# A third layer issued in program order on four engines, with the ends of its passes spread over the steps that follow

## Chip, core and metric

One Trainium2 chip, one core. The metric is the device time of one execution in microseconds (us). Before any experiment the kernel before took 2380.44 us (median of 3 runs, 2375.94 to 2380.57). Stage lengths come from the profiled execution of each kernel, times and ratios from all of its runs.

## The reference, cut to what matters

Four layers work on 4096 nodes of 128 features with a full 4096 x 4096 matrix `adj`; each adds to x and normalises it. The change concerns the third layer, an attention with four heads, and the product with `adj` that starts the fourth.

```python
def _L2_gnn_ref(x, adj_matrix, weight, att_src, att_dst, bias):      # third layer
    ...
    C = alpha_src[None, :, :] + alpha_dst[:, None, :]
    adj_t = adj_matrix.T[..., None]
    tau = adj_t * jnp.exp(jnp.maximum(0.2 * C, C))
    tau_sum = jnp.sum(tau, axis=1, keepdims=True)
    att_weights = tau / tau_sum
    z = jnp.einsum('mnh,nhf->mhf', adj_t * att_weights, h_prime)
    return z.reshape(n, heads * f_out) + bias

def _L3_gnn_ref(h, adj, W_self, W_neigh):                            # fourth layer
    deg = jnp.clip(jnp.sum(adj, axis=1, keepdims=True), 1.0)
    h_neigh = adj @ h / deg
    return h @ W_self + h_neigh @ W_neigh
...
    x = _layernorm(x + _L2_gnn_ref(...), axis=-1)
    x = _layernorm(x + _L3_gnn_ref(...), axis=-1)
```

The denominators are sums of tau; the numerators need adj * tau, that is, a second factor of `adj`. Both are products on TensorE.

## The kernel before

The third layer takes the targets in four strips of 1024 (`WB`) and the heads in two pairs: eight passes of 32 steps (`NT`), 128 source nodes a step. (PSUM, below, is the memory in which the results of matmuls stand; the other tiles lie in SBUF.) One step, and the end of a pass:

```python
def attention(l2w, bufs, mp, hp):
    D = []                                            # targets: TensorE spreads them into PSUM
    ...
    for nt in range(NT):
        ...                                           # every second step loads a chunk of adj
        nc.scalar.activation(sq, a[:, 0:OWN], AF.Square)
        for h in range(2):
            nc.vector.scalar_tensor_tensor(tau[:, h, :], D[h], E(h), a, op0=ALU.max, op1=ALU.mult)
        nc.vector.scalar_tensor_tensor(tau2[:, 0, 0:OWN], D[0][:, 0:OWN], E(0), sq,
                                       op0=ALU.max, op1=ALU.mult)                # the 704-wide one
        nc.gpsimd.tensor_tensor(tau2[:, 0, OWN:WB], tau[:, 0, OWN:WB], a[:, OWN:WB], ALU.mult)
        nc.gpsimd.tensor_tensor(tau2[:, 1, :], tau[:, 1, :], a, ALU.mult)
        product(den, nt, tau, True)                   # four matmuls, each on 32 columns
        late.append((nt, tau2))
        if len(late) > 1:
            product(num, *late.pop(0), False)         # numerators one step behind
        yield
    ...                                               # end of the pass: copy, transpose, divide, add to x
```

One matmul of the fourth layer's product (a "piece") is put into each step, and whatever a strip needs at its end is written down in one lump:

```python
for mp in range(NW):
    for hp in range(H // 2):
        if (mp, hp) != (0, 0):                        # pass 0 runs inside the second layer
            for _ in attention(l2w, 3, mp, hp):
                next(pieces, None)
    for _ in pieces:
        pass
    for j in (2 * mp, 2 * mp + 1):
        layer3_block(j)                               # layer norm of the strip, blocks for the product
    pieces = layer3_product(mp)
for _ in pieces:
    pass
```

A scheduler then decides in which order each engine takes its instructions.

## Time and profile before

I cut every profile at the same events: the start of VectorE's 704-wide instruction, which stands once in every step. "Pass 0 ends" is the start of the last one of pass 0; the "edge" runs from there to the first one of pass 1; the "passes" from there to the last one of pass 7; the "tail" from there to the end of the span.

| kernel before | us |
|---|---|
| pass 0 ends | 1482.8 |
| edge from pass 0 to pass 1 | 8.1 |
| passes 1 to 7 (224 steps) | 796.8 |
| tail | 88.6 |
| profiled span | 2376.4 |

### The profile page before, as it was taken

What the parts mean: (1) busy time and instruction counts of PE and PEld (TensorE: products, weight loads), DVE (VectorE), ACT (ScalarE), POOL (GpSimd) and SP (SyncE); (2) the same over time, 40 slices, a digit from 0 to 9 for tenths busy, and PEclk for the clock granted to TensorE, in tenths of its full rate; (3) what the DMA queues carried; (4) which work ended last, traced back from release to release, by engine and by line L of the source; (5) the groups of instructions that cost most, each with busy time, mean ns of one, the idle gap of its engine ahead of it and who ended that gap; (6) DMA issues with size and microseconds to landing.
All of it is one profiled execution on the core that took longest, in us unless ns stands there. A gap on an engine that the chain in (4) does not pass through costs nothing.

```text
span 2376.4 us, 23290 instructions
## 1 busy us (share of the span) xinstructions
PE 2247.5 (95%) x8798; PEld 860.8 (36%) x8798; DVE 1371.0 (58%) x1981; ACT 484.2 (20%) x716; POOL 847.5 (36%) x541
## 2 busy tenths in 40 slices
PE   5899999999999999999999998879998999999988
PEld 3334444444444444444433332112222222222233
DVE  4443458777110110000156656999799999999965
ACT  5665000000000000000122121223222222322220
POOL 0000000000000000000043424999698899889950
PEclk8899999999999999999999998999999999999999
DMA  9988888999878778888877774446665666666655
GB/s 363 347 274 263 246 246 263 290 294 291 263 243 264 233 233 261 280 263 258 262 256 235 266 265 160 146 156 229 213 213 195 209 216 231 212 217 229 220 193 188
DMA packets 261802, 575.39 MB, mean 242 GB/s; under 512 B 9776, under 2 KB 15920, under 8 KB 261680
## 3 DMA queue, kind: packets, MB, share of 16 engines
q1 hardware_dynamic: 252352, 566.27, 73.3%
q10 hardware_dynamic: 9328, 7.54, 1.0%
q8 instruction: 71, 1.16, 0.2%
q14 instruction: 51, 0.42, 0.1%
HBM read 571.67 MB, written 2.10 MB: 241 GB/s over the span
## 4 chain that ended last, share of the span: by engine, by line
PE 83%; DVE 9%; DMA 4%; issue 2%; ACT 1%; POOL 1%; DVEq 0%; ACTq 0%; POOLq 0%
PE pacc L455 27%; PE pacc L319 10%; PE den L607 10%; PE pp L677 10%; PE pp L712 10%; PE num L607 7%; DVE tau L623 5%; DMA chunk<-in_adjT 3%; PE pmm L496 2%; PE num L677 1%; PE px L103 1%; PE pden L305 1%; DVE tau L624 1%; PE ptr L314 1%; PE px L663 1%
## 5 line engine op out<-in xcount | busy, mean ns | idle before, releaser
L623 DVE SCALAR_TENSOR_TENSOR tau<-d,es,chunk 128x1024 f32<-128x1024 f32 x512 | 634.9, 1277 | 25.1 <-issue 16.2
L627 POOL TENSOR_TENSOR tau<-tau,chunk 128x1024 f32<-128x1024 f32 x256 | 611.4, 2388 | 54.8 <-DVE tau L623 47.1
L607 PE MATMUL den<-tau,cs 128*32 128x512 f32 x2048 | 457.5, 605 | 8.6 <-DVE tau L623 8.1
L585 POOL TENSOR_TENSOR x<-x,B2R 128x512 f32<-128x512 f32 x8 | 10.1, 1268 | 1245.1 <-PE px L103 1245.1
L607 PE MATMUL num<-tau,hc 128*32 128x512 f32 x2048 | 413.8, 601 | 32.1 <-POOL tau L627 27.6
L618 ACT ACTIVATE sq<-chunk 128x704 f32<-128x704 f32 x256 | 201.5, 791 | 605.6 <-DVE tau L624 528.9
L626 POOL TENSOR_TENSOR tau<-tau,chunk 128x320 f32<-128x320 f32 x256 | 226.0, 883 | 115.7 <-PE num L607 46.9
L319 PE MATMUL pacc<-chunk,hw 128*128 128x512 f32 x512 | 254.8, 635 | 3.0 <-DVE hw L352 3.0
L677 PE MATMUL pp<-chunk,xT 128*128 128x512 f32 x448 | 243.5, 637 | 11.8 <-DMA chunk<-in_adjT 11.4
L624 DVE SCALAR_TENSOR_TENSOR tau<-d,es,sq 128x704 f32<-128x704 f32 x256 | 241.8, 944 | 18.9 <-PE num L607 14.1
L712 PE MATMUL pp<-chunk,w 128*128 128x512 f32 x512 | 235.6, 602 | 1.2 <-DVE t2T L718 1.2
L455 PE MATMUL pacc<-chunk,x 128*128 128x512 f32 x512 | 223.6, 594 | 0.0
L455 PE MATMUL pacc<-chunk,t 128*128 128x512 f32 x512 | 223.6, 592 | 0.0
L455 PE MATMUL pacc<-chunk,v 128*128 128x512 f32 x512 | 221.4, 592 | 0.0
L607 PEld LDWEIGHTS num<-tau,hc 128*32 128x32 f32 x2048 | 82.2, 109 | 248.2 <-POOL tau L627 83.5
L607 PEld LDWEIGHTS den<-tau,cs 128*32 128x32 f32 x2048 | 86.0, 108 | 222.3 <-issue 106.0
L299 DVE TENSOR_SCALAR pos<-chunk 128x2048 bf16<-128x2048 f32 x92 | 110.8, 1222 | 75.4 <-DMA chunk<-in_adjT 69.6
L517 DVE COPY w<-ptr 128x512 f32<-128x512 f32 x8 | 5.5, 692 | 246.1 <-PE ptr L515 246.1
L455 PEld LDWEIGHTS pacc<-chunk,v 128*128 128x128 f32 x512 | 97.1, 190 | 121.5 <-issue 121.5
L455 PEld LDWEIGHTS pacc<-chunk,t 128*128 128x128 f32 x512 | 96.1, 190 | 114.8 <-issue 114.8
L712 PEld LDWEIGHTS pp<-chunk,w 128*128 128x128 f32 x512 | 92.2, 190 | 124.6 <-issue 117.7
L455 PEld LDWEIGHTS pacc<-chunk,x 128*128 128x128 f32 x512 | 95.8, 190 | 113.4 <-issue 113.4
(171 smaller groups left out, 1461.1 us busy)
## 6 DMA issues: line engine op xcount, KB each, us to landing
chunk<-in_adjT SPq DMA_DIRECT2D x412, 1024.0 KB, 5.5
chunk<-in_adj SPq DMA_DIRECT2D x128, 1024.0 KB, 5.3
xT<-in_xT ACTq DMA_DIRECT2D x8, 256.0 KB, 6.6
out<-o ACTq DMA_DIRECT2D x8, 256.0 KB, 3.6
W1A<-in_w1a ACTq DMA_DIRECT2D x1, 384.0 KB, 3.5
W1B<-in_w1b ACTq DMA_DIRECT2D x1, 384.0 KB, 4.4
W0T<-in_w0gT ACTq DMA_DIRECT2D x1, 64.0 KB, 4.0
W<-in_w0g ACTq DMA_DIRECT2D x1, 64.0 KB, 6.5
```

The costliest lines, as they stand in the source:

```text
L299: nc.vector.tensor_scalar(pos, a, 0.0, None, op0=ALU.is_gt)
L319: nc.tensor.matmul(p, hw[:, j * TB + k, :], a[:, k, :], start=first and k == 0, stop=last and k == TB - 1)
L455: nc.tensor.matmul(p, stationary(c * TB + k), a[:, k, :], start=n == 0 and k == 0, stop=n == NB - 1 and k == TB - 1)
L496: nc.tensor.matmul(ph, W1A[:, k, hh * P:(hh + 1) * P], r, start=k == 0, stop=k == 2)
L607: nc.tensor.matmul(acc[q:q + 32, :], weights(nt, 2 * hp + h, is_den), r[:, h, mb * IB:(mb + 1) * IB], start=nt == 0, stop=nt == NT - 1)
L618: nc.scalar.activation(sq, a[:, 0:OWN], AF.Square)
L623: nc.vector.scalar_tensor_tensor(tau[:, h, :], D[h], E(h), a, op0=ALU.max, op1=ALU.mult)
L624: nc.vector.scalar_tensor_tensor(tau2[:, 0, 0:OWN], D[0][:, 0:OWN], E(0), sq, op0=ALU.max, op1=ALU.mult)
L626: nc.gpsimd.tensor_tensor(tau2[:, 0, OWN:WB], tau[:, 0, OWN:WB], a[:, OWN:WB], ALU.mult)
L627: nc.gpsimd.tensor_tensor(tau2[:, 1, :], tau[:, 1, :], a, ALU.mult)
L677: nc.tensor.matmul(p, y[:, (2 * mp + c) * TB + k, :], a[:, k, :], start=c == 0 and k == 0, stop=c == 1 and k == TB - 1)
L712: nc.tensor.matmul(p, w[:, c * TB + k, :], a[:, k, :], start=c == 0 and k == 0, stop=c == NB - 1 and k == TB - 1)
```

## The change

Its intent: VectorE is to work without a hole through the seven passes. Four engines take their instructions in program order; denominators are multiplied one step behind, numerators two; the stages that end a pass become generators, of which one stage is issued per step of the next pass; the matmuls of the product are dealt out by a credit. The core of the diff, cut:

```diff
+            with tc.manual_schedule(engines={PE, DVE, Activation, Pool}):       # names shortened
+                chains = deque([heads.finish()])
+                pieces = deque()
+                credit = rate = 0.0
...
+                for s, (mp, hp, nt) in enumerate(steps):
+                    if nt == 0:
+                        heads.targets()
+                    a, sq = ahead
+                    tau, tau2 = heads.step(nt, l2w, (3, 4), a, sq)
+                    if s + 1 < len(steps):
+                        ahead = passes[steps[s + 1][:2]].squares(steps[s + 1][2], l2w, 3)
+                    behind.append((heads, nt, tau, tau2))
+                    if len(behind) > 1:
+                        before = behind[-2]
+                        before[0].product(True, before[1], before[2])
+                    if len(behind) > 2:
+                        before = behind.popleft()
+                        before[0].product(False, before[1], before[3])
+                        if before[1] == NT - 1:
+                            ...                # queue the pass end, the strip's layer norm, its product
+                    credit = min(credit + rate, 2.0)
+                    while credit >= 1.0:
+                        credit -= 1.0
+                        if one(pieces):
+                            credit = 0.0
+                    one(chains)
...
-                            if k < TB - 1:
-                                yield
-                        if c == 0:
-                            yield
+                            yield c == 1 and k == TB - 1
...
-                    yield
+                    yield True
...
+                nc.vector.scalar_tensor_tensor(tau[:, 0, :], D[0], E(nt, 0), a, op0=ALU.max, op1=ALU.mult)
+                nc.gpsimd.tensor_tensor(tau2[:, 0, OWN:WB], tau[:, 0, OWN:WB], a[:, OWN:WB], ALU.mult)
+                nc.vector.scalar_tensor_tensor(tau2[:, 0, 0:OWN], D[0][:, 0:OWN], E(nt, 0), sq,
+                                               op0=ALU.max, op1=ALU.mult)
+                nc.vector.scalar_tensor_tensor(tau[:, 1, :], D[1], E(nt, 1), a, op0=ALU.max, op1=ALU.mult)
+                nc.gpsimd.tensor_tensor(tau2[:, 1, :], tau[:, 1, :], a, ALU.mult)
```

The layer norm now takes a strip of eight 128-node tiles at once (`layer3_blocks`):

```python
nc.vector.tensor_scalar_add(s, mv[:, tb, 1], LN_EPS)
nc.scalar.activation(s, s, AF.Sqrt)
yield
nc.vector.reciprocal(s, s)
nc.vector.scalar_tensor_tensor(m, mv[:, tb, 0], -1.0, s, op0=ALU.mult, op1=ALU.mult)
```

## The prediction

> **What bounds the kernel now.** I read the page for the engines' shares, then the table by stretches cut at the edges of the attention passes, then the timeline inside one pass, at one edge between passes and after the last pass. The page names TensorE, but its busy time alone does not settle who sets the pace.
>
> ```profile
> PE 2247.5 (95%) x8798; PEld 860.8 (36%) x8798; DVE 1371.0 (58%) x1981; ACT 484.2 (20%) x716; POOL 847.5 (36%) x541
> L627 POOL TENSOR_TENSOR tau<-tau,chunk 128x1024 f32<-128x1024 f32 x256 | 611.4, 2388 | 54.8 <-DVE tau L623 47.1
> ```
>
> The third layer has eight passes (four target strips, two head pairs) of 32 steps. A step is three VectorE instructions (two tau of 128x1024, one squared part of 128x704), two GpSimd products, four denominator and four numerator matmuls. Pass 0 runs inside the second layer; passes 1 to 7 are the stretches from 1491 to 2288; the last product follows.
>
> ```profile
> core 0: us, PE busy (x) PEld busy (x) DVE busy (x) ACT busy (x) POOL busy (x), PEclk, DMA share, GB/s
> 1137.00:1454.00 317.00, 313.77 (x1087) 121.16 (x1091) 169.38 (x286) 64.36 (x110) 104.30 (x63) 0.99 0.77 254
> 1491.00:1592.00 101.00, 84.21 (x498) 16.03 (x500) 101.00 (x94) 24.51 (x31) 99.78 (x63) 1.00 0.49 156
> 1592.00:1714.00 122.00, 113.82 (x600) 29.89 (x596) 108.28 (x121) 36.20 (x59) 102.25 (x66) 0.99 0.61 209
> 1714.00:1829.00 115.00, 103.13 (x602) 26.96 (x604) 105.78 (x99) 28.22 (x38) 104.21 (x68) 1.00 0.65 217
> 1829.00:1949.00 120.00, 115.43 (x618) 31.29 (x614) 110.88 (x124) 33.25 (x54) 104.04 (x67) 0.99 0.60 204
> 1949.00:2059.00 110.00, 107.52 (x591) 26.89 (x584) 107.15 (x103) 26.40 (x34) 103.85 (x66) 1.00 0.66 229
> 2059.00:2178.00 119.00, 114.44 (x618) 31.37 (x616) 112.25 (x126) 33.36 (x54) 104.65 (x68) 1.00 0.64 214
> 2178.00:2288.00 110.00, 107.54 (x590) 27.02 (x588) 107.17 (x103) 25.62 (x33) 103.86 (x67) 1.00 0.66 227
> 2288.00:2376.00 88.00, 71.82 (x208) 32.81 (x202) 41.12 (x180) 10.07 (x30) 2.26 (x1) 0.92 0.53 170
> ```
>
> To see: pass 1, without pieces of the last product, has VectorE busy all of its 101 us. The other six take 110 to 122 us for about the same VectorE work. VectorE sums to 752.5 of 797 us over the seven, so **44.5 us of idle VectorE** is what reordering can win there. Before 1454 TensorE is full (313.8 of 317); after 2288 it idles 16 of 88 us.
>
> ```profile
> 1533.04 0.95 DVE L624 SCALAR_TENSOR_TENSOR tau<-d,es,sq 128x704 f32<-128x704 f32 x1
> 1533.20 2.37 POOL L627 TENSOR_TENSOR tau<-tau,chunk 128x1024 f32<-128x1024 f32 x1
> ...
> 1536.28 0.95 DVE L624 SCALAR_TENSOR_TENSOR tau<-d,es,sq 128x704 f32<-128x704 f32 x1
> ```
>
> A step is 3.24 us: 1.19 + 1.19 + 0.86 from start to start (the printed 1277 and 944 ns contain an end that overlaps the next). GpSimd needs 2.33 + 0.82 = 3.15 us, nearly the same.
>
> ```profile
> 1713.87 0.95 DVE L624 SCALAR_TENSOR_TENSOR tau<-d,es,sq 128x704 f32<-128x704 f32 x1
> 1722.37 1.28 DVE L623 SCALAR_TENSOR_TENSOR tau<-d,es,chunk 128x1024 f32<-128x1024 f32 x1 [7.56 <-issue]
> ```
>
> An edge between passes: VectorE stands 7.6 us. From the last 704-wide instruction of a pass to the first of the next it is 8.1, 6.3, 12.3, 6.5, 6.4, 6.3 and 6.4 us, where 3.24 would be one step. Inside passes 2, 4 and 6 there are more holes, early, where the layer norm and the blocks for the product are made.
>
> ```profile
> 2287.74 0.94 DVE L624 SCALAR_TENSOR_TENSOR tau<-d,es,sq 128x704 f32<-128x704 f32 x1
> ...
> 2302.00 2.07 PE L677 MATMUL pp<-chunk,xT 128*128 128x512 f32 x2 [0.46 <-ACT xT L665]
> ```
>
> From the last step's 704-wide instruction to the end: 88.6 us, of which 14.3 until the last strip's product starts.
>
> **What the Trainium skill says.** "PSUM — Partial Sum Buffer", Engine vs sequencer instructions: the Vector, Scalar and GpSimd queues are strict FIFO, and matmuls start and complete in program order. So one waiting instruction holds all behind it, and the order in which work is written into a queue is what can change here; the 7.6 us agree, as there was enough other VectorE work later in its queue. "TensorE: Matmul & The Clock Gate", Part 3, The mechanism: matmuls at different tile positions overlap. The trace agrees: eight denominator records begin at 1452.14 and the next product at 1453.02, so a product of four 32-column matmuls costs 0.88 us, about what one full-width fp32 matmul costs (two records, 0.43 us apart). "Perfetto Trace Analysis", Optimization Strategy: regimes with different bounds may gain by interleaving; strewing the pass ends over the next steps does that.
>
> **The change part by part.** No arithmetic is removed: the same products, adds and copies. The manual order covers the seven passes on four engines.
>
> *The passes.* VectorE's order in a step becomes tau 0, squared part, tau 1; denominators are multiplied one step behind, numerators two. Then TensorE needs only results of finished VectorE steps: 1.84 us for both products (4 x 0.43 plus start) and about 0.96 us for a piece, 2.8 of 3.24. VectorE then needs 223 x 3.24 = 722.5 us from the first to the last 704-wide instruction, plus what cannot leave it: seven pass ends at 0.77 (5.4), three layer norms at 2.3 (6.9), 13 accumulator adds at 0.60 (7.8), in all 742.6. The busy sum without the three adds that move to the tail gives 750.7. I take 748, some small waits included, against 796.8 now: **-49 us**.
>
> *Edge from pass 0 to pass 1.* The new targets now go between the last products, so 8.1 becomes about 0.86 + 1.19 + 1.5 wait + 1.19 = 4.7: **-3.4 us**.
>
> *Pass 0.* It stays outside the manual order but takes the new step order, and the listed TensorE order is more chopped: denominators of one head, one numerator, denominators of the other. Counting how many matmuls fall on the same 32 columns within each unbroken group, 86 rounds instead of 78 stand between the second layer's products; 8 x 0.86 = 6.9 us on an engine that is full there. Some may fall into its 3 us of idle: **+5 us**.
>
> *The tail.* This is what the rate in the diff decides. A piece of the product is one matmul; a block is eight and one add. The credit is set to zero after the eighth matmul and after the add, so a rate of 1.14 gives nine steps for a block, not 7.9, and 72 steps for a strip where 64 exist. Dealt out by this rule, strip 0 starts at step 49, strip 1 at 121, strip 2 at 189 of 224; even with 1.6 (seven steps a block) **24 matmuls of strip 2 remain**. The listed TensorE order confirms it: after the last numerators three groups of eight, and among them the transposes of the last pass end. From the last 704-wide instruction: tau 1 ends at 2.1, GpSimd at 4.5, last numerators at 5.6 us; three groups of 8 x 0.86 = 6.9 us with a waiting add and transposes between them (0.9 each) reach 28.3; transposes, copy and weights up to the first new piece take 3.8 as now (2298.2 to 2302.0); from there to the end 74.4 as now. Sum 106.5 against 88.6: **+17.9 us**.
>
> Sum: -49 - 3.4 + 5 + 17.9 = -29.5; 2380.4 - 29.5 = **2351 us**, -1.2%.
>
> **Rivals.** *GpSimd or TensorE takes VectorE's place.* GpSimd has 0.09 us to spare in a step, and each pass end gives it 1.4 us more; TensorE with two pieces has 3.7 us for a 3.24 us step. For it: these margins, and a fixed order cannot go round a late result. Against: buffers of three and four steps and two steps of lag let both recover, and over seven steps with eight pieces TensorE needs 20.5 of 22.7 us. If it happens, 10 to 20 us of the 49 go: 2361 to 2371. *The loads.* Six chunk buffers are shared, and a chunk waiting for its buffer holds later ones; the queue already waits mostly for GpSimd and for the pieces. A buffer is used some 4 to 5 steps and comes round after about 8, so a load has some 10 us for 5.5. I give late loads up to 10 us. *The remaining pieces hide.* TensorE idles 16 us after 2288 and the pieces are 20.6 us; fully hidden, the tail grows by only 5 us: 2338. Against: the transposes stand behind them in one queue. *Pass 0 costs nothing:* 2346.
>
> **Range and chances.** Full success in the passes and a costless pass 0 give about 2342; the tail hidden as well, 2333, just the 2% line (2332.8). Stalls of 20 us give 2371. I set 2339 to 2368. Faster by over 2% needs every rival to fall my way: 0.06. Slower by over 2% would need a stall in nearly every step: 0.02. Within 2%: 0.92.
>
> **What would show it.** Steps of 3.24 us in all seven passes and edges under 5 us; VectorE over 97% busy from the first to the last of them; 24 product matmuls (48 records) between the last numerators and the last strip's layer norm; a tail near 106 us; a slightly longer second layer. I am wrong if steps are longer with VectorE waiting for TensorE, GpSimd or a load, or if the tail stays below 95 us.

## More of the kernel before

The next lines are the totals of VectorE's waits over the edge and the passes. Columns: what waited, what it waited for, us in total, how many times, the longest.

```profile
DVE tau L623 <- issue: 16.2, 16, 7.6
DVE acc L686 <- PE pp L677: 7.6, 2, 4.0
DVE rd L639 <- PE px L103: 7.5, 7, 3.1
DVE tau L623 <- PE den L607: 5.6, 5, 2.3
DVE tau L624 <- PE num L607: 4.1, 5, 1.4
```

No single wait carries the loss. The pieces of the pass ends (rd), the accumulator (acc) and the products (den, num) each hold VectorE for a few us. The largest entry, "issue", has no releaser that this view shows, but 10.9 of its 16.2 us are the starts of passes 2 to 7, and the timelines give their cause: at all six the first tau starts 0.1 us after TensorE has made the targets that it reads. At the start of pass 3:

```profile
1721.67 0.60 PE L597 MATMUL d<-dv,selD 96*128 96x512 bf16 x2
1722.37 1.28 DVE L623 SCALAR_TENSOR_TENSOR tau<-d,es,chunk 128x1024 f32<-128x1024 f32 x1 [7.56 <-issue]
```

TensorE comes to the targets late because it first works off products of earlier steps and three pieces, one of which waited 1.63 us for its chunk of `adj` (1714.68).

## The result, and the profile after

The kernel after takes **2354.68 us** (median of 4 runs, 2353.51 to 2358.86), the kernel before 2379.89 us on the same chip (4 runs, 2375.94 to 2380.57). The ratio is 0.9901 with a 95% interval of 0.9883 to 0.9918. Here and below a ratio is the mean time of one kernel's fast runs over that of the other's of the same rounds, so it is not quite the ratio of the medians that I quote.

| stage (us) | before | after | difference | predicted |
|---|---|---|---|---|
| pass 0 ends | 1482.8 | 1485.5 | +2.7 | +5 |
| edge 0 to 1 | 8.1 | 10.0 | +1.9 | -3.4 |
| passes 1 to 7 | 796.8 | 756.9 | -40.0 | -49 |
| tail | 88.6 | 104.7 | +16.1 | +17.9 |
| span | 2376.4 | 2357.1 | -19.3 | -29.5 |

The stages show less than the times, -19.3 against -25.2 us by the medians, because the profiled execution of the kernel after (2358.86 us) is the slowest of its four, and that of the kernel before (2378.27 us) is 1.6 us below the median.

First the line of engine shares of the kernel after. TensorE's share has hardly moved, though the same 8798 matmul records stand in a shorter span: its busy time fell from 2247.5 to 2219.8 us. This line does not say what happened.

```profile
PE 2219.8 (94%) x8798; PEld 877.1 (37%) x8798; DVE 1380.5 (59%) x1969; ACT 480.3 (20%) x712; POOL 844.8 (36%) x541
```

Then the table by stretches of the kernel after (us; busy us and instruction counts of PE, weight load, VectorE, ScalarE, GpSimd; granted clock; DMA share; GB/s): passes 1 and 2, all seven passes, and the tail.

```profile
1495.00:1597.00 102.00, 71.65 (x490) 16.67 (x488) 101.51 (x96) 26.14 (x34) 98.41 (x63) 0.98 0.46 147
1597.00:1711.00 114.00, 101.98 (x592) 29.65 (x592) 113.35 (x120) 34.03 (x55) 106.84 (x69) 0.99 0.55 183
...
2253.00:2357.00 104.00, 91.28 (x268) 41.21 (x262) 43.67 (x181) 9.90 (x29) 3.91 (x3) 0.97 0.65 211
1495.00:2253.00 758.00, 697.10 (x4042) 197.68 (x4042) 754.42 (x753) 204.76 (x302) 721.09 (x459) 1.00 0.63 210
```

The last line is the one to read: VectorE is busy 754.42 of 758 us, where it was busy 752.51 of 797. Its work is the same, its idle time went from 44.5 to 3.6 us. All of its waits that are left, over the edge and the passes:

```profile
DVE tau L620 <- PE d L610: 3.4, 1, 3.4
DVE tau L622 <- ACT sq L602: 3.2, 1, 3.2
DVE tau L620 <- POOL tau L621: 2.1, 5, 0.8
```

The last entry bears GpSimd's name, but its five waits are the starts of passes 3 to 7, and each ends 0.1 us after the targets are made (1709.93 and 1710.03 at the first); at the start of pass 7 GpSimd's product had ended 0.8 us before. So these too are waits for the targets.

An edge between passes, here from pass 1 to pass 2 in VectorE's timeline of the kernel after. The stop of 7.56 us of the kernel before is gone; the step across the edge takes 3.24 us like any other (1596.66 to 1599.91).

```profile
1596.66 0.94 DVE L622 SCALAR_TENSOR_TENSOR tau<-d,es,sq 128x704 f32<-128x704 f32 x1
1597.52 1.28 DVE L624 SCALAR_TENSOR_TENSOR tau<-d,es,chunk 128x1024 f32<-128x1024 f32 x1
1598.71 1.28 DVE L620 SCALAR_TENSOR_TENSOR tau<-d,es,chunk 128x1024 f32<-128x1024 f32 x1
1599.91 0.94 DVE L622 SCALAR_TENSOR_TENSOR tau<-d,es,sq 128x704 f32<-128x704 f32 x1
```

TensorE's timeline in the tail of the kernel after. The last 704-wide instruction starts at 2252.35.

```profile
2257.97 7.13 PE L709 MATMUL pp<-chunk,xT 128*128 128x512 f32 x16
2264.94 0.49 PE L104 MATMUL px<-ident,nd 128*128 128x128 f32 x3
2265.89 7.13 PE L709 MATMUL pp<-chunk,xT 128*128 128x512 f32 x16 [0.46 <-DVE acc L715]
2272.86 0.60 PE L104 MATMUL px<-ident,nd 128*128 128x128 f32 x4
2273.80 7.13 PE L709 MATMUL pp<-chunk,xT 128*128 128x512 f32 x16 [0.34 <-DVE acc L715]
2280.77 0.60 PE L104 MATMUL px<-ident,x 128*128 128x128 f32 x4
2282.05 1.13 PE L693 MATMUL px<-W,xb 128*128 128x256 f32 x4 [0.67 <-ACT xb L687]
2283.64 1.12 PE L709 MATMUL pp<-chunk,xT 128*128 128x512 f32 x2 [0.46 <-ACT xT L695]
```

These are the 24 matmuls (48 records) of strip 2 that the credit left over, with the transposes of the last pass caught between them. The last strip's product starts 31.3 us after the last 704-wide instruction (2283.64 - 2252.35), where it started 14.3 us after it before.

**Where the passes kept 9 us that I expected to go.** Almost every step is 3.24 us, but three steps in each strip's layer norm take 4.8, 5.7 and 5.7. Two VectorE instructions on 128x8 elements are far longer than their size asks. VectorE's timeline there:

```profile
1628.63 0.83 DVE L674 TENSOR_SCALAR rstd<-mv 128x8 f32<-128x8 f32 x1
...
1632.84 2.31 DVE L678 SCALAR_TENSOR_TENSOR mean<-mv,rstd 128x8 f32<-128x8 f32 x1
1635.08 1.27 DVE L620 SCALAR_TENSOR_TENSOR tau<-d,es,chunk 128x1024 f32<-128x1024 f32 x1
```

And GpSimd's in the same us:

```profile
1627.07 2.36 POOL L625 TENSOR_TENSOR tau<-tau,chunk 128x1024 f32<-128x1024 f32 x1 [1.04 <-DVE tau L624]
...
1632.77 2.36 POOL L625 TENSOR_TENSOR tau<-tau,chunk 128x1024 f32<-128x1024 f32 x1 [1.13 <-DVE tau L624]
```

Each of the two small instructions ends within 0.03 us of the GpSimd product that was running when it started: 1629.46 beside 1629.43, and 1635.15 beside 1635.13. The Trainium skill states the mechanism under "SBUF — State Buffer", Who interferes with whom: VectorE (there DVE) shares one pair of ports with GpSimd, "A DVE instruction with two SBUF inputs contends with a GpSimd instruction that reads SBUF", and whoever comes second waits for the whole instruction. The mean product has two inputs in SBUF (mv and rstd). It is issued right after the tau that releases the GpSimd product, so in a fixed order it meets that product in each of the three strips. In the tail, with GpSimd idle, the same instruction took 0.17 us.

**The edge from pass 0 to pass 1** became longer: VectorE waits 3.4 us for the targets and 3.2 us for the first square. ScalarE's timeline shows why the square is late. It stands behind two copies, and the first of them waits 16.25 us for the last denominators.

```profile
1492.02 0.58 ACT L642 COPY nd<-den 128x512 f32<-128x512 f32 x1 [16.25 <-PE den L637]
1494.12 0.58 ACT L642 COPY nd<-num 128x512 f32<-128x512 f32 x1 [1.52 <-PE num L637]
1494.61 2.15 ACT L602 ACTIVATE sq<-chunk 128x704 f32<-128x704 f32 x3
```

### The profile page after: what moved, and what is told of

The parts are those of the page before. It is cut to its first block, busy times and chain, and to the rows that moved or that the text cites. A ratio compares the mean times of both kernels' runs of the same rounds, so it can differ in the third digit from the quotient of the medians.

```text
span 2357.1 us, 23237 instructions
## 1 busy us (share of the span) xinstructions
PE 2219.8 (94%) x8798; PEld 877.1 (37%) x8798; DVE 1380.5 (59%) x1969; ACT 480.3 (20%) x712; POOL 844.8 (36%) x541
## 5 line engine op out<-in xcount | busy, mean ns | idle before, releaser
L637 PE MATMUL den<-tau,cs 128*32 128x512 f32 x2048 | 401.2, 609 | 61.7 <-DVE tau L624 55.6
L581 POOL TENSOR_TENSOR x<-x,B2R 128x512 f32<-128x512 f32 x8 | 10.2, 1270 | 1240.0 <-PE px L104 1240.0
L637 PE MATMUL num<-tau,hc 128*32 128x512 f32 x2048 | 380.1, 598 | 4.3 <-POOL tau L625 3.6
L620 DVE SCALAR_TENSOR_TENSOR tau<-d,es,chunk 128x1024 f32<-128x1024 f32 x256 | 326.6, 1276 | 7.9 <-PE d L610 4.1
L624 DVE SCALAR_TENSOR_TENSOR tau<-d,es,chunk 128x1024 f32<-128x1024 f32 x256 | 327.1, 1278 | 0.1
L622 DVE SCALAR_TENSOR_TENSOR tau<-d,es,sq 128x704 f32<-128x704 f32 x256 | 241.8, 945 | 13.4 <-PE num L637 10.0
L709 PE MATMUL pp<-chunk,xT 128*128 128x512 f32 x448 | 236.2, 629 | 1.3 <-DVE acc L715 0.8
L637 PEld LDWEIGHTS den<-tau,cs 128*32 128x32 f32 x2048 | 65.6, 107 | 312.5 <-DVE tau L624 170.5
L637 PEld LDWEIGHTS num<-tau,hc 128*32 128x32 f32 x2048 | 93.1, 110 | 151.8 <-issue 135.3
```

Of the source, the lines that this page charges most:

```text
L620: nc.vector.scalar_tensor_tensor(tau[:, 0, :], D[0], E(nt, 0), a, op0=ALU.max, op1=ALU.mult)
L624: nc.vector.scalar_tensor_tensor(tau[:, 1, :], D[1], E(nt, 1), a, op0=ALU.max, op1=ALU.mult)
L637: nc.tensor.matmul(acc[q:q + 32, :], weights(nt, 2 * self.hp + h, is_den), r[:, h, mb * IB:(mb + 1) * IB], start=nt == 0, stop=nt == NT - 1)
L709: nc.tensor.matmul(p, y[:, (2 * mp + c) * TB + k, :], a[:, k, :], start=c == 0 and k == 0, stop=c == 1 and k == TB - 1)
```

## The experiments

All runs gave the right result. The runs came in three batches; in those the kernel before took 2379.92, 2380.40 and 2379.05 us (medians). The stages of each profiled execution, cut as above:

| kernel | pass 0 ends | edge 0 to 1 | passes | tail | span | time (median) | ratio to before |
|---|---|---|---|---|---|---|---|
| before | 1482.8 | 8.1 | 796.8 | 88.6 | 2376.4 | 2379.89 | 1 |
| after | 1485.5 | 10.0 | 756.9 | 104.7 | 2357.1 | 2354.68 | 0.9901 |
| e1_credit_kept | 1485.3 | 10.0 | 762.6 | 93.9 | 2351.9 | 2351.94 | 0.9878 |
| e2_small_off_vector | 1488.4 | 8.3 | 749.9 | 104.5 | 2351.1 | 2351.90 | 0.9881 |
| e3_scheduler_order | 1481.1 | 8.3 | 830.9 | 103.8 | 2424.1 | 2428.81 | 1.0213 |
| e4_ends_at_once | 1482.7 | 8.3 | 806.4 | 99.5 | 2396.9 | 2397.31 | 1.0078 |
| e5_no_lag | 1486.3 | 7.8 | 789.5 | 104.3 | 2387.9 | 2387.18 | 1.0021 |
| e6_pass0_old_step | 1481.2 | 5.4 | 756.9 | 105.0 | 2348.5 | 2346.56 | 0.9853 |
| e7_first_square | 1482.4 | 5.1 | 756.9 | 104.9 | 2349.2 | 2350.28 | 0.9867 |
| e8_norm_in_psum | 1479.1 | 8.3 | 748.7 | 105.0 | 2341.2 | 2345.43 | 0.9862 |
| c1_together | 1480.5 | 5.4 | 750.7 | 94.5 | 2331.2 | 2333.82 | 0.9801 |
| c2_together_psum | 1482.3 | 5.4 | 751.6 | 94.4 | 2333.8 | 2335.72 | 0.9809 |

A warning on the first column: pass 0 is left to the scheduler, which orders it anew for every kernel, so kernels with the same code for pass 0 differ there by up to 9 us (1479.1 to 1488.4), and the edge behind it is 8.3 us in e2, e4 and e8, whose edits leave it as it is in the kernel after (10.0). A difference in the total is therefore credited to a change only where its own stage moved.

A second warning: the 704-wide instruction stands behind both tau in the old order of a step and between them in the new one, that is, one tau or 1.2 us earlier. So from before to after, 1.2 us move from "pass 0 ends" into the tail, and with the old step in pass 0 (e6, c1, c2) 1.2 us move from the edge to "pass 0 ends". Sums of stages are not touched by this.

### e1: the credit is kept after a block

```diff
-                            yield c == 1 and k == TB - 1
+                            yield False
```

> Only the reset of the credit after a block's eighth matmul is taken out (the reset after the add stays), so the product of strip 2 fits into the steps: the listed order has 1 matmul left after the last numerators where the changed kernel has 24. Theory (the remaining matmuls are paid in full at the end): the tail from the last 704-wide instruction goes from 104.8 to about 89 us, the passes lengthen by under 5 us, the time falls by 12 to 16 us to about 2341 us. Rival (the reset protects TensorE from waiting for the accumulator add, or two matmuls a step make it the bound): the passes of the last strip lengthen by 10 us or more and the time stays within 5 us of the changed kernel's.

Measured: 2351.94 us, ratio 0.9878 (0.9862 to 0.9895). The tail lost 10.8 us and the passes got 5.7 us. So the credit rule does leave the three groups to the tail, and taking them out of it pays about half back by the stages. In the time it is 2.7 us by the medians, where 12 to 16 were expected, and the intervals of the two ratios overlap: the gain is shown in the stages, not in the time. The passes pay for three more accumulator adds (3 x 0.6 us), and for VectorE waiting on the product, a wait that the kernel after did not have:

```profile
DVE acc L715 <- PE pp L709: 3.7, 7, 2.1
```

The tail does not shrink to 88.6 because TensorE is behind when the passes end: the first transposes of the last pass start at 2264.52, 6.6 us after the last 704-wide instruction (2257.96); in the kernel before they start 1.95 us after it (1.2 us of the difference is the second tau, see the second warning).

### e2: the two small instructions of the layer norm leave VectorE

```diff
-                nc.vector.tensor_scalar_add(s, mv[:, tb, 1], LN_EPS)
-                nc.scalar.activation(s, s, AF.Sqrt)
+                nc.scalar.activation(s, mv[:, tb, 1], AF.Sqrt, bias=eps)
 ...
-                nc.vector.scalar_tensor_tensor(m, mv[:, tb, 0], -1.0, s, op0=ALU.mult, op1=ALU.mult)
+                nc.gpsimd.tensor_tensor(m, mv[:, tb, 0], s, ALU.mult)
+                nc.gpsimd.tensor_scalar(m, m, -1.0, None, op0=ALU.mult)
```

> The two small layer-norm instructions that took 0.83 and 2.31 us on VectorE are taken off it: the add of epsilon goes into ScalarE's square root as a bias, the product for the mean goes to GpSimd (two small instructions). Theory (VectorE stands in these two because GpSimd is in a long product; both ended when GpSimd's did): the three steps of a strip's layer norm go from 4.8, 5.7 and 5.7 us to about 4.8, 4.9 and 3.5, in all -9 us, time about 2346 us. Rival (they are slow because they wait for results just written, the wait goes along with the work): ScalarE's normalisation gets its bias later and no step becomes shorter by over 0.5 us, time unchanged.

Measured: 2351.90 us (2346 expected), ratio 0.9881 (0.9865 to 0.9898); the passes lost 7.0 us, while pass 0, which the edit leaves alone, ended 2.9 us later. The three steps are now 4.8, 4.9 and 3.3 us. Not all of it was won, because the mean now stands behind GpSimd's own product (GpSimd's timeline):

```profile
1633.19 2.38 POOL L627 TENSOR_TENSOR tau<-tau,chunk 128x1024 f32<-128x1024 f32 x1 [1.13 <-DVE tau L626]
1635.53 0.21 POOL L679 TENSOR_TENSOR mean<-mv,rstd 128x8 f32<-128x8 f32 x1
```

The normalisation on ScalarE then starts later, the next square behind it is late, and VectorE waits (its timeline):

```profile
1638.45 0.95 DVE L624 SCALAR_TENSOR_TENSOR tau<-d,es,sq 128x704 f32<-128x704 f32 x1 [0.85 <-ACT sq L604]
```

This run shows that the two instructions cost the time, not yet why they are long. That is asked in e8.

### e3: the new program, but the scheduler orders it

```diff
-            with tc.manual_schedule(engines={PE, DVE, Activation, Pool}):       # names shortened
+            with ExitStack():
```

> The changed code without the manual order: the automatic scheduler orders the engines again, all else as changed (step order, lags, strewn ends, rate). Theory (the fixed order closes the holes): edges between passes go back to 6 us and more and the first steps of passes 2, 4 and 6 have holes again, passes 780 to 800 us instead of 757, time 2378 to 2400. Rival (the order in which the program is written is what counts and the scheduler follows it): passes within 5 us of 757, time within 8 us of the changed kernel's.

Measured: 2428.81 us, ratio 1.0213 (1.0196 to 1.0230), slower than the kernel before. The passes, 830.9 us, are longer than the 780 to 800 expected: the strewn stages without the fixed order lose 34 us there even against before. VectorE's waits in e3, the three longest:

```profile
DVE tau L620 <- issue: 33.4, 15, 6.0
DVE tau L620 <- PE den L637: 27.1, 19, 3.7
DVE tau L620 <- POOL tau L625: 12.0, 4, 3.3
```

### e4: the fixed order, but each pass end is issued in one step

```diff
-                    one(chains)
+                    while chains:
+                        one(chains)
```

> Manual order kept, but the work that ends a pass is all written into one step instead of one portion in each. Theory (in a strict queue each portion must stand where its input is ready, so strewing is needed): VectorE waits in the reciprocal and in the product after it about 5 us at each of seven pass ends, and some 9 us more at three layer norms, passes about 60 us longer, time about 2415 us. Rival (three and four buffers and the slack of 0.4 us in each step absorb it): under 15 us longer.

Measured: 2397.31 us, ratio 1.0078 (1.0056 to 1.0100); the passes take 49.5 us more than in the kernel after and 10 us more than before. The edges between passes are still 3.2 to 4.7 us. Some 42 of the 49.5 us lie at the three norms (two steps of 10.5 and 16.5 us, where the kernel after has three of 4.8, 5.7 and 5.7), where VectorE waits for squares. The expectation came near the size (60 us) but named other waits: those for the reciprocal and the product after it come to 7.5 us in all. The largest entry:

```profile
DVE tau L622 <- ACT sq L602: 42.9, 4, 13.4
```

The squares stand in ScalarE's queue behind the normalisation and the copies of the strip's blocks, and the copies wait for TensorE again and again, up to 2.2 us each. The Trainium skill, "PSUM — Partial Sum Buffer", Engine vs sequencer instructions, says that ScalarE's queue is strict FIFO; three waits of 13.1 to 13.4 us, one for each strip, are what it costs here when a stage of several engines is issued at once (the fourth, 3.2 us, is the edge from pass 0). So neither half of the change gains alone: against the kernel before, the order without the strewing loses 17.4 us and the strewing without the order 48.9 us (differences of the medians of the same batch). In the passes alone they lose some 10 and 34 us; the rest is the tail, some 11 and 15 us longer, which comes from the credit rule in each of these kernels.

### e5: no second step of lag

```diff
                     behind.append((heads, nt, tau, tau2))
+                    before = behind[-1]
+                    before[0].product(True, before[1], before[2])
                     if len(behind) > 1:
-                        before = behind[-2]
-                        before[0].product(True, before[1], before[2])
-                    if len(behind) > 2:
                         before = behind.popleft()
                         before[0].product(False, before[1], before[3])
```

> Denominators are multiplied in their own step and numerators one step behind, instead of one and two steps behind; everything else as in the kernel after. Theory A (the lag carries the edges): the targets of a new pass stand in TensorE's queue behind products that wait for the step's own results, so VectorE waits some 3 us more at each of the six edges between passes, and TensorE has less slack in the steps; edges of 6 to 7 us instead of 3.2 to 4.2, passes some 20 us longer, about 2375 us. Theory B (only the order of the pass ends counts): steps stay at 3.24 us and edges at 3.2 to 4.2, less than 5 us of difference, about 2355 us.

Measured: 2387.18 us, ratio 1.0021 (0.9998 to 1.0043): without the lag the whole gain in time is gone. (The passes are still 7 us shorter than in the kernel before; the tail of the credit rule takes that back.) The six edges between passes take 5.9 to 7.9 us instead of 3.2 to 4.2, which is 19.5 of the 32.6 us by which the passes grew. VectorE's largest wait:

```profile
DVE tau L620 <- issue: 18.8, 5, 4.6
```

It is the edge of the kernel before again, and again the targets are late: at all six edges the first tau that reads them starts 0.1 us after they are made (1714.67 and 1714.77 at the first of these five; the sixth wait, 2.6 us, is listed under GpSimd). This is theory A's mechanism. The other 13 us lie in single steps that take 3.7 to 5.3 us; waits for squares come to 4.2 us in eight places. I expected the edges, not these.

### e6: pass 0 with the step of before

```diff
-                        tau, tau2 = heads.step(nt, l2a, (2, 2), *heads.squares(nt, l2a, 2))
+                        tau, tau2 = heads.old_step(nt, l2a, (2, 2), *heads.squares(nt, l2a, 2))
```

`old_step` issues both tau before the 704-wide instruction, as the kernel before does.

> Pass 0, inside the second layer, gets the instruction order of a step that the kernel before has; the seven passes after it are as in the kernel after. Theory A (my prediction: the new step order chops the products of pass 0 and costs rounds on a full TensorE): the last 704-wide instruction of pass 0 comes 3 to 7 us earlier than the 1485.5 of the kernel after, near 1482 or less, and the time falls as much, about 2351 us. Theory B (TensorE's idle time takes the rounds up, or they do not exist): the end of pass 0 moves by less than 2 us, the time stays at 2355 us.

Measured: 2346.56 us (2351 expected), ratio 0.9853 (0.9833 to 0.9873). Pass 0 ends 4.3 us earlier, the edge is 4.6 us shorter (5.5 and 3.4 by the second warning), passes and tail are unchanged. Neither theory had the edge: ScalarE's copies of pass 0's results now start at 1482.53 and 1484.90 and the first square at 1485.38, in time for VectorE (1486.63), so the wait for it is gone. The end of pass 0 alone would not prove it, as the scheduler moves it (see above). A narrower measure does: the time from the first to the last start of the second layer's third set of big products, the ones that pass 0 is threaded through. It is 314.6, 313.0, 310.8 and 313.0 us in the kernels with the old step there (before, e6, c1, c2) and 316.4 to 320.3 us in the eight with the new one (318.6 in the kernel after). The two groups do not overlap; their means are 312.9 and 318.0 us. The clock granted there was 0.995 in before, e2 and e5 and 1.00 in the others; at 1.00 alone it is 310.8 to 313.0 against 316.4 to 318.6. The new step order costs some 5 us on a full TensorE.

### e7: the first square of pass 1 ahead of the copies

```diff
+                    heads.ahead = Heads(0, 1)                     # before pass 0's last numerators
+                    heads.first = heads.ahead.squares(0, l2a, 1, xT[:, 0:OWN])
 ...
-                ahead = passes[steps[0][:2]].squares(0, l2w, 3)
+                passes[0, 1] = heads.ahead
+                ahead = heads.first
```

> The first square of pass 1 is issued before the last numerators of pass 0, into a place that is free by then, so that it stands ahead of the two copies of numerators and denominators in ScalarE's queue. Theory A: the 3.2 us that VectorE waits there for the square go, the edge from pass 0 to pass 1 shrinks from 10.0 to about 6.8 us, time about 2351.5 us. Theory B: another wait takes its place (the targets behind the numerators, GpSimd), the edge stays at 10 us and the time at 2355 us.

Measured: 2350.28 us, ratio 0.9867 (0.9846 to 0.9888). The edge went from 10.0 to 5.1 us. Of VectorE's waits there, the one for the square (3.2 us) is gone, as theory A had it. The one for the targets is 1.8 us instead of 3.4, but it is 1.7 to 1.8 us in e2, e4 and e8 too, so this part is not e7's. The rest of the difference in the span (3.1 us at the end of pass 0) is within what the scheduler moves.

### e8: the same small instructions, one operand in PSUM

The instructions stay on VectorE, at the same place and beside the same GpSimd products; only where an operand lies changes.

```diff
-                nc.vector.tensor_scalar_add(s, mv[:, tb, 1], LN_EPS)
-                nc.scalar.activation(s, s, AF.Sqrt)
+                q = ps_x.tile([P, 2 * TB], F32, name="px")
+                nc.vector.tensor_scalar_add(q, mv[:, tb, 1], LN_EPS)
+                nc.scalar.activation(s, q, AF.Sqrt)
                 yield
+                q = ps_x.tile([P, 2 * TB], F32, name="px")
+                nc.vector.reciprocal(q, s)
                 nc.vector.reciprocal(s, s)
-                nc.vector.scalar_tensor_tensor(m, mv[:, tb, 0], -1.0, s, op0=ALU.mult, op1=ALU.mult)
+                nc.vector.scalar_tensor_tensor(m, mv[:, tb, 0], -1.0, q, op0=ALU.mult, op1=ALU.mult)
```

> The two small instructions of the layer norm stay on VectorE, at the same place in its queue and beside the same GpSimd products, but one operand of each lies in PSUM instead of SBUF: the variance with its addend is written to PSUM, and the mean is multiplied by a reciprocal in PSUM (one more reciprocal of about 0.1 us). Theory A (VectorE and GpSimd exclude each other where VectorE needs two ways into SBUF): 0.83 and 2.31 us become about 0.2 each, the steps of a layer norm 4.8, 5.7 and 5.7 us become 4.8, about 5.0 and 3.6, the passes lose about 8 us of 756.9, time near 2347 us. Theory B (these instructions are long for another reason, for instance because they wait for a result or because of their place behind the statistics): they stay at 0.8 and 2.3 us, the passes at 757 us, time 2355 us.

Measured: 2345.43 us, ratio 0.9862 (0.9847 to 0.9877); the passes lost 8.1 us, and the three steps take 4.8, 5.1 and 3.6 us. VectorE's timeline:

```profile
1620.56 0.17 DVE L675 TENSOR_SCALAR px<-mv 128x8 f32<-128x8 f32 x1
...
1624.27 0.11 DVE L681 SCALAR_TENSOR_TENSOR mean<-mv,px 128x8 f32<-128x8 f32 x1
```

GpSimd's in the same us:

```profile
1619.01 2.37 POOL L625 TENSOR_TENSOR tau<-tau,chunk 128x1024 f32<-128x1024 f32 x1 [1.02 <-DVE tau L624]
...
1624.08 2.38 POOL L625 TENSOR_TENSOR tau<-tau,chunk 128x1024 f32<-128x1024 f32 x1 [1.14 <-DVE tau L624]
```

Both GpSimd products run throughout, in all three strips, and the two instructions take 0.17 and 0.11 us instead of 0.83 and 2.31. A queue place or a late result would have kept them long. The counterpart is in e4: there both instructions are as in the kernel after, GpSimd happens to stand still beside them, and each takes 0.17 us. So it is GpSimd's use of SBUF that they waited for. (The rest of this run's advantage in the span, 6.4 us at the end of pass 0 and 1.7 at the edge, is in stages that the edit does not touch.)

### c1 and c2: the parts together

c1 joins e1, e2, e6 and e7, with two small additions: a variance is aggregated after the next tile's statistics have been issued, and the stages of a norm are divided anew, so that the mean has a step of its own before the normalisation:

```diff
-                        stats(x[:, t, :], t)
+                        st = small.tile([P, 6], F32, name="st")
+                        nc.vector.bn_stats(st, x[:, t, :])
+                        if last:
+                            nc.vector.bn_aggr(mv[:, last[0], :], last[1])
+                        last = t, st
+                    nc.vector.bn_aggr(mv[:, last[0], :], last[1])
 ...
+                yield                                             # after the mean
 ...
-                    yield
+                    if j == 0:
+                        yield
```

> All that the runs so far point to in one kernel: credit kept after a block (no strip left for the tail), the small instructions of the layer norm off VectorE with a step between the mean and the normalisation, bn_stats issued one ahead of bn_aggr, the old step order in pass 0, the first square of pass 1 issued early. If the effects add: tail 11 us shorter than in the kernel after but three adds and some waits back in the passes (-3 to -5 net), layer norms -7 to -9, statistics -3, pass 0 -3, edge -3: about 2333 us, with 2325 to 2345 likely; ratio to before near 0.98. If they do not add, because the same VectorE time is counted twice or GpSimd and TensorE become the bound: 2345 to 2352 us.

Measured: **2333.82 us** (median of 5, 2332.92 to 2334.31), ratio 0.9801 (0.9784 to 0.9818). It beats both kernels. Against the kernel after (20.9 us by the medians), pass 0 ends 5.0 us earlier, the edge is 4.6, the passes 6.2 and the tail 10.2 us shorter; together 25.9 = 2357.1 - 2331.2. Pass 0 and the edge are no better than in e6 alone, so e6 and e7 cure the same delay (the late first square) and do not add. The statistics steps are 4.4 and 4.4 us where e2 has 4.8 and 4.9. What VectorE still waits for longest is the product:

```profile
DVE acc L739 <- PE pp L733: 8.4, 8, 4.7
```

c2 differs from c1 only in the mean, which is made on VectorE with an operand in PSUM, as in e8.

> As the kernel with all changes together, but the mean is multiplied on VectorE by a reciprocal in PSUM instead of by two GpSimd instructions. If theory A of the run before it holds, the mean comes about 2.4 us earlier and GpSimd is spared 0.45 us at each norm; VectorE gets 0.3 us more at each. I expect the same time within 3 us, about 2332 us; if theory B holds, 6 us more, about 2340 us.

Measured: 2335.72 us (2331.81 to 2336.54), ratio 0.9809 (0.9795 to 0.9822). The intervals of c1 and c2 overlap; the two ways of avoiding the collision are worth the same here, and both kernels are the fastest of all.

## Why the prediction was right or wrong

The time was predicted at 2351 us and is 2354.68, inside the range and within 2% of before, as expected. The closeness is in part luck: the passes and the first edge fell short of their terms by 14.3 us, and 4.1 us came back from pass 0 and the tail, whose losses were smaller than predicted. By its steps:

**The bound: right.** VectorE set the pace, and 40.9 of its 44.5 idle us were won. Neither GpSimd, TensorE nor the loads took its place; of the first rival 2.1 us are left (the targets at the starts of passes 3 to 7), the second does not appear among VectorE's waits. One reading was wrong: the 7.6 us at the edge were put down to the order in VectorE's own queue. VectorE waited for targets that stood late in TensorE's order, and without the lag of the products this comes back (e5).

**The passes: right in mechanism, the layer norms mis-sized.** The failed term is "three layer norms at 2.3 (6.9)". The three steps of a norm exceed 3 x 3.24 us by 6.5 us, 19.5 us for the three strips. The rest fits: 756.9 less 722.5 for the steps and 19.5 for the norms leaves 14.9 us, where pass ends and accumulator adds were put at 13.2 and 2.1 us of waiting is seen. I had taken the small instructions at the sizes they mostly have in the trace of before (medians of 0.17 and 0.15 us, though the same view has longest ones of 1.6 us, which I left out). The collision was in that trace: the two means that took 1.6 us, at 1841.72 and 2072.11, end 0.02 us after the GpSimd product beside them, and the six others, with no such product beside them, take 0.15 us. In the kernel after they cost 0.83 and 2.31 us because a fixed order sets them beside a GpSimd product every time; e8 shows it. The statistics are the other part: in program order a pair of instructions comes every 0.39 us, which is 3.1 us for the eight tiles of a strip and alone more than my 2.3. The pitch was 0.26 us where other work or another tile lies between them, as in c1 (1612.92, 1613.18, 1613.44).

**Edge from pass 0: wrong, no gain.** It is 10.0 us here and 8.3 in three runs with the same code for it, against 8.1 before. I counted a wait for the targets (1.5 us; it is 3.4 here and 1.8 there) and did not look at ScalarE, where the first square stands behind two copies that wait for the last products. e7 removes that wait and gets 5.1 us, near the 4.7 predicted.

**Pass 0: right.** +5 was predicted; the end moved by 2.7 in this pair of profiles, or 3.9 at the same place in the step, and the stretch of products by 4.0 (318.6 against 314.6). (The prediction counts the 1.2 us of the second tau in the tail and does not take them off here; put right, its sum is -30.7.) e6 shortens the stretch by 5.6 us. That the cause is the count of rounds of 0.86 us was my reading of the order; no run varied the rounds alone.

**The tail: right, to 1.8 us.** The 24 matmuls, their three groups (7.1 us each, 6.9 predicted) and the transposes between them are in the trace as described; 104.7 us against 106.5 predicted. The rival that the pieces hide in TensorE's idle time fell. e1 shows the limit of the step: keeping the credit wins back 10.8 us of the tail, not all of the 16, and costs 5.7 in the passes.

What stays open: whether the count of rounds is what the new step costs pass 0, and how far the spread of pass 0 is the scheduler's choice and how far it varies from run to run.

## What to carry to other kernels

When the order of a queue is fixed by hand, read each queue of every engine that the bound engine depends on, not only its own: here one square behind two copies in ScalarE's queue cost VectorE 3.2 us at one edge. A small VectorE instruction with two SBUF inputs, put right behind the instruction that releases a long GpSimd product, waits for nearly that whole product (2.31 of 2.36 us); one operand in PSUM or another engine avoids it. And a fixed order, lag between the engines and spread-out stage ends are one change: with any one of the three taken out the kernel was no faster than the kernel before (e3, e4, e5).

## What the Trainium skill lacked or had wrong

- "SBUF — State Buffer", Who interferes with whom: right, and the prediction, which did not draw on it, would have been nearer with it. It gives the rule without its price for a small instruction: 0.17 us became 2.31 us for 128x8 elements, the rest of a GpSimd product of 2.36 us. It says that an instruction with at most one SBUF input, outside the modes that use both ports, does not contend, but not that putting an operand in PSUM gets one there (0.11 us beside a running product).
- The same section, on the instruction with one SBUF input that adds a constant: it may collide when it runs in a mode that uses both ports. The collision is in the trace (0.83 us beside GpSimd, 0.17 us with its result in PSUM); which mode it ran in, no run here shows.
- No page that I found gives the cost of the statistics instructions: a pair of them on 128x128 elements comes every 0.39 us when each aggregate directly follows its own statistics, and every 0.26 us when another tile's statistics lie between.
- "PSUM — Partial Sum Buffer", Engine vs sequencer instructions, names the strict FIFO of the queues; it has no example of its cost across engines. Here the copies of a stage issued at once, ahead of a square in ScalarE's queue, held VectorE 13.4 us (e4).
- "TensorE: Matmul & The Clock Gate", Part 3, says that matmuls at different tile positions overlap, not what mixing two products of such matmuls costs: with the new order of a step in place of the old one the same products took 318.6 instead of 313.0 us of a full TensorE (the kernel after and e6, clock 1.00 in both).
